# Output stage of three selective-scan layers: two passes with tokens on partitions in place of three stages with channels on partitions

## The chip, the cores and the metric

The kernel runs on one core of a Trainium2 chip. Its work is spread over five engines that take their instructions in order and wait for each other by semaphores: TensorE (PE in the profile, its weight loads PEld), VectorE (DVE), ScalarE (ACT), GpSimd (POOL) and SyncE (SP), which here issues all DMA transfers. The metric is the device time of one execution in microseconds (us). The kernel before was run three times outside the profiler.

## What is computed

The input is four images of 64 x 64 tokens with 192 channels, all float32. Four residual layers follow each other. Each normalizes the image by groups of channels, runs a selective state-space scan in one or four directions, and adds its result to the image. Layers b, c and d (the reference's L1, L2, L3) end alike. This is the part that the change touches, here of layer d (the sum is over its four directions; layer b has one):

```python
xz = jnp.einsum('bhwc,dc->bhwd', x, in_proj_w)
xc, z = jnp.split(xz, 2, axis=-1)
...
y = y1 + inv2 + wh + invwh
y = jnp.transpose(y, (0, 2, 1)).reshape(b, h, w, D_INNER)
mu = jnp.mean(y, axis=-1, keepdims=True)
var = jnp.var(y, axis=-1, keepdims=True)
y = (y - mu) * jax.lax.rsqrt(var + EPS) * ln_gamma + ln_beta
y = y * silu(z)
return jnp.einsum('bhwd,cd->bhwc', y, out_proj_w)
```

The layer norm runs over the 384 inner channels (192 in layer c) of each token. Layer b reverses every second row of the image before its scan and again behind it ("snake"). Layer a has no layer norm and an output stage of its own (`out0`), which stays as it is.

## The kernel before, in words

`net` (L961) takes the images one after the other and each through the layers a, b, c, d, so the output stage of `layer` (L893) runs 12 times. An image has L = 4096 tokens, cut into NCH = 8 chunks of T = 512; a chunk is TB = 4 blocks of 128 tokens. Inner channels lie in nb blocks of P: 3 x 128 in layers b and d, 2 x 96 in layer c.

`layer` first loads the image and convolves it, then `scans` (L274) makes the states and writes each direction's output to HBM with tokens in rows (`store`, L605: `yo`). The output stage reads these back in three stages, each with tile pools of its own:

- `gather` (L685): for each chunk it loads the 512 tokens of every direction (L693, tiles `yi`, tokens on partitions), and PE turns them by transposes that add up in PSUM (L699), 4 per block and direction. ACT or DVE copy the sum to `y` (L706 to L711), with channels on partitions; the snake is undone in that copy.
- `layernorm` (L713): the mean over channels is a sum over partitions, so PE multiplies with a matrix of 1/n (L722, `mean_w` of L54 to L58). DVE subtracts it (L725), ACT squares (L726), PE makes the mean of squares (L729), `rsqrt` (L77) takes Ln and Exp on ACT (L81, L82) and one Newton step of four DVE operations (L83 to L86), on 128 x 512 elements per chunk. DVE multiplies by gamma and by the result (L735).
- `gate_out` (L739): loads the image again (L746), `normalize` (L118, operation at L121), PE projects the gate z (L753), ACT takes Silu (L757), DVE adds beta and multiplies (L758), PE projects out (L765), DVE adds the image (L769), SP stores (L770). Its weights are loaded at L947 to L951.

Every float32 matmul of 512 columns stands in the trace as two records; every transpose as one.

The program text is not the order of execution on an engine. A scheduler of the tile framework orders each engine's instructions beforehand from its own estimate of when they can run, and adds the waits; `keep` (L261) pins the order inside the scans, and `behind` (L61) makes an instruction follow given others. A tile with `bufs=2` has two buffers in turn, and the third user waits for the first to be done. A new pool's first user waits for all that used that memory before.

Of the kernel before, what the change touches and what calls it, by code (L numbers as in the profile page):

```python
# [16 lines left out]
L = H * W  # L17
# [22 lines left out]
def rows(ap):  # L40

    return ap.rearrange("p (r w) -> p r w", w=W)


class Net:
    def __init__(self, tc, d, const):
        self.tc, self.nc, self.d = tc, tc.nc, d
        self.pinned = {}
        nc = self.nc
        self.ident = const.tile([128, 128], F32, tag="ident", name="ident")  # L50
        make_identity(nc, self.ident)
        self.gmat = const.tile([HP, HP], F32, tag="gmat", name="gmat")
        nc.sync.dma_start(self.gmat, d["gmat"])
        self.mean_w = {}  # L54
        for p, n in ((128, 384), (96, 192)):
            m = const.tile([p, p], F32, tag=f"mean{n}", name=f"mean{n}")
            nc.vector.memset(m, 1.0 / n)
            self.mean_w[n] = m  # L58
# [626 lines left out]
    def gather(self, pool, pp, y, outs, P, nb, snake, key):  # L685

        nc = self.nc
        for ch in range(NCH):
            s = slice(ch * T, (ch + 1) * T)
            yt = []  # L690
            for i, o in enumerate(outs):
                t = pool.tile([128, TB, nb * P], F32, tag=f"yt{i}", bufs=2, name=f"yi_{key}{ch}{i}")
                nc.sync.dma_start(t, o[s].rearrange("(q p) c -> p q c", p=128))  # L693
                yt.append(t)
            for b in range(nb):
                ps = pp.tile([P, T], F32, tag="py", bufs=2, name=f"pg_{key}{ch}{b}")
                for i, t in enumerate(yt):
                    for q in range(TB):
                        nc.tensor.matmul(  # L699
                            ps[:, q * 128 : (q + 1) * 128], t[:, q, b * P : (b + 1) * P], self.ident,  # L700
                            start=i == 0 and q == 0, stop=i == len(yt) - 1 and q == TB - 1,
                            is_transpose=True,
                        )
                o, ps = rows(y[:, b, s]), rows(ps)
                if snake:
                    nc.scalar.copy(o[:, 0::2, :], ps[:, 0::2, :])  # L706
                    nc.scalar.copy(o[:, 1::2, ::-1], ps[:, 1::2, :])
                elif b % 2:
                    nc.vector.tensor_copy(o, ps)
                else:  # L710
                    nc.scalar.copy(o, ps)  # L711

    def layernorm(self, pool, pp, y, P, nb, gamma, key):  # L713

        nc = self.nc
        ones = self.mean_w[P * nb]
        for ch in range(NCH):
            s = slice(ch * T, (ch + 1) * T)
            k = f"{key}{ch}"
            pm = pp.tile([P, T], F32, tag="pm", bufs=2, name=f"pm_{k}")  # L720
            for b in range(nb):
                nc.tensor.matmul(pm, ones, y[:, b, s], start=b == 0, stop=b == nb - 1)  # L722
            sq = pool.tile([P, nb, T], F32, tag="sq", bufs=2, name=f"sq_{k}")
            for b in range(nb):
                nc.vector.tensor_tensor(y[:, b, s], y[:, b, s], pm, ALU.subtract)  # L725
                nc.scalar.activation(sq[:, b, :], y[:, b, s], AF.Square)  # L726
            pv = pp.tile([P, T], F32, tag="pv", bufs=2, name=f"pv_{k}")
            for b in range(nb):
                nc.tensor.matmul(pv, ones, sq[:, b, :], start=b == 0, stop=b == nb - 1)  # L729
            v = pool.tile([P, T], F32, tag="v", bufs=2, name=f"v_{k}")  # L730
            nc.vector.tensor_scalar(v, pv, LN_EPS, None, ALU.add)
            r = pool.tile([P, T], F32, tag="r", bufs=2, name=f"r_{k}")
            self.rsqrt(pool, r, v, [P, T], k)
            for b in range(nb):
                nc.vector.scalar_tensor_tensor(  # L735
                    y[:, b, s], y[:, b, s], gamma[:, b, :], r, ALU.mult, ALU.mult
                )

    def gate_out(self, pool, pp, y, P, nb, wz, wo, beta, x_src, norm, dst, key):  # L739

        nc = self.nc
        for ch in range(NCH):
            s = slice(ch * T, (ch + 1) * T)
            k = f"{key}{ch}"
            x = pool.tile([HP, 2, T], F32, tag="gx", bufs=3, name=f"gx_{k}")
# [3 lines left out]
            o = pool.tile([P, nb, T], F32, tag="go", bufs=2, name=f"go_{k}")  # L749
            for b in range(nb):  # L750
                pz = pp.tile([P, T], F32, tag="pz", bufs=3, name=f"pz_{k}{b}")
                for h in range(2):
# [3 lines left out]
                z = pool.tile([P, T], F32, tag="gz", bufs=3, name=f"gz_{k}{b}")  # L756
                nc.scalar.activation(z, pz, AF.Silu)  # L757
                nc.vector.scalar_tensor_tensor(  # L758
                    o[:, b, :], y[:, b, s], beta[:, b, :], z, ALU.add, ALU.mult
                )  # L760
            res = pool.tile([HP, 2, T], F32, tag="gr", bufs=3, name=f"gr_{k}")
            for h in range(2):
                po = pp.tile([HP, T], F32, tag="po", bufs=2, name=f"po_{k}{h}")
                for b in range(nb):
                    nc.tensor.matmul(  # L765
                        po, wo[:, b, h * HP : (h + 1) * HP], o[:, b, :],
# [126 lines left out]
    def layer(self, name, x_src, dst, dp, P, nb, dirs, snake, twice):  # L893
# [5 lines left out]
        with tc.tile_pool(name=f"{name}_keep", bufs=1) as keep, ExitStack() as late:  # L899
# [154 lines left out]
```

## Time and profile before

| what | us |
|---|---|
| three runs, median (lowest to highest) | 35676.95 (35669.4 to 35704.8) |
| the profiled execution's own time | 35697.36 |
| span of the program in that execution | 35695.6 |
| output stage of layer b, four images: last transposed sum of the scan to last addition of L769 | 205.1, 206.1, 206.3, 208.9 |
| layer c, the same | 173.6, 175.3, 173.4, 173.6 |
| layer d, the same | 247.6, 248.0, 248.2, 246.8 |
| sum of these twelve | 2512.9 |
| mean granted TensorE clock over the span | 0.813 |

A profile shows one execution. Per group of equal instructions it gives the time they kept the engine busy, the mean of one in ns, and the idle time just before them with what ended it. A view by windows gives each engine's busy time in stretches of the span; beside it "PEclk" is the share of full clock that TensorE was granted, "DMA share" the mean busy share of the 16 DMA engines. A timeline lists instructions by start; runs of the same kind are merged ("x12"). A view of one source line gives shortest, median and longest duration of what this line issued. "a<-b,c" reads: written a, read b and c.

### The profile page before, as it was taken

To read this page: it belongs to the slowest core of one execution; us is meant where nothing else is said; L and a number is where in the kernel's file an instruction comes from. 1 tells how busy PE (TensorE), PEld (TensorE's weight loads), DVE (VectorE), ACT (ScalarE), POOL (GpSimd) and SP (SyncE) were. 2 spreads that over 40 slices of the span, in tenths; PEclk is the share of its full clock that TensorE was granted. 3 is DMA by queue.
4 is the path that set the end of the run, shared out by engine and by line. 5 is a ranking of instruction groups with operands and counts; after the bars stand their busy time and mean duration, and the time that the engine had idled before them with its cause. 6 is when DMAs were issued, how large, how long until landed. Compare 5 with 4: busy or idle time off the path is not lost. (4 is left out here: it accounts for less than half of the span.)

```text
span 35695.6 us, 396533 instructions
## 1 busy us (share of the span) xinstructions
PE 25702.0 (72%) x138688; PEld 18685.0 (52%) x138688; DVE 28265.2 (79%) x22866; ACT 24090.2 (67%) x45011; POOL 25347.8 (71%) x10978
## 2 busy tenths in 40 slices
PE   7778777666777877766677787776667778777666
PEld 4554454554455445455445544545544554454555
DVE  7885697887788569788778856978877885697887
ACT  6773585775677358577667735857766773585776
POOL 6883595896688359588668835958866883595886
PEclk8888877878888877787888887778788888777878
DMA  3332233223333223322333322332233332233223
GB/s 107 106 106 76 76 106 89 93 95 103 105 106 105 76 75 106 89 92 95 103 106 107 105 76 76 106 89 92 95 102 106 106 106 76 75 106 90 93 95 101
DMA packets 1354910, 3405.80 MB, mean 95 GB/s; under 512 B 185696, under 2 KB 633040, under 8 KB 1346768
## 3 DMA queue, kind: packets, MB, share of 16 engines
q1 hardware_dynamic: 1352912, 3380.43, 30.1%
q8 instruction: 1099, 18.01, 0.2%
q14 instruction: 899, 7.36, 0.1%
HBM read 2924.88 MB, written 455.08 MB: 95 GB/s over the span
## 5 line engine op out<-in xcount | busy, mean ns | idle before, releaser
L600 PE MATMUL py_d<-ident,c_d 128*128 128x128 f32 x24576 | 3823.1, 314 | 2138.6 <-POOL c_d L582 1307.7
L600 PE MATMUL py_a<-ident,c_a 128*128 128x128 f32 x24576 | 3635.0, 302 | 2212.5 <-POOL c_a L582 1143.6
L582 POOL TENSOR_TENSOR c_d<-h_d,C_d 128x1024 f32<-128x1024 f32 x2036 | 4777.0, 2366 | 163.2 <-DVE h_d L565 160.6
L582 POOL TENSOR_TENSOR c_a<-h_a,C_a 128x1024 f32<-128x1024 f32 x1908 | 4479.3, 2371 | 418.0 <-issue 284.2
L600 PEld LDWEIGHTS py_d<-ident,c_d 128*128 128x128 f32 x24576 | 3369.2, 164 | 2590.2 <-POOL c_d L582 1627.4
L600 PEld LDWEIGHTS py_a<-ident,c_a 128*128 128x128 f32 x24576 | 3155.4, 157 | 2522.0 <-DVE c_a L582 1267.7
L527 POOL TENSOR_TENSOR u_d<-du_d,B_d 128x1024 f32<-128x1024 f32 x1536 | 3618.4, 2360 | 900.0 <-issue 886.4
L527 POOL TENSOR_TENSOR u_a<-du_a,B_a 128x1024 f32<-128x1024 f32 x1536 | 3606.5, 2363 | 716.2 <-DVE h_a L558 696.5
L582 POOL TENSOR_TENSOR c_c<-h_c,C_c 96x1024 f32<-96x1024 f32 x1356 | 3179.2, 2361 | 383.4 <-DVE h_c L565 371.5
L565 DVE TENSOR_TENSOR_SCAN h_d<-dA_d,carry_d,u_d 128x512 f32<-128x512 f32 x2536 | 3073.3, 1264 | 333.3 <-POOL c_d L582 263.0
L519 ACT ACTIVATE dA_d<-delta_d,A_d 128x512 f32<-128x512 f32 x3072 | 2118.2, 690 | 1637.6 <-DVE c_d L582 1491.9
L519 ACT ACTIVATE dA_a<-delta_a,A_a 128x512 f32<-128x512 f32 x3072 | 2120.3, 690 | 1244.9 <-DVE c_a L582 1089.1
L600 PE MATMUL py_c<-ident,c_c 96*128 96x96 f32 x16384 | 2233.3, 303 | 867.3 <-DVE c_c L582 666.5
L558 DVE TENSOR_TENSOR_SCAN h_a<-dA_a,u_a 128x1024 f32<-128x1024 f32 x1140 | 2579.4, 2281 | 332.0 <-ACT dA_a L523 179.0
L600 PEld LDWEIGHTS py_c<-ident,c_c 96*128 96x128 f32 x16384 | 2025.9, 181 | 1196.9 <-DVE c_c L582 789.2
L527 POOL TENSOR_TENSOR u_c<-du_c,B_c 96x1024 f32<-96x1024 f32 x1024 | 2412.3, 2362 | 6.3 <-DVE dA_c L565 6.0
L544 PE MATMUL ut_d<-ident,dut_d 128*128 128x128 f32 x12288 | 1911.4, 307 | 631.5 <-DVE c_d L582 605.6
L536 ACT ACTIVATE dut_a<-duT_a,BT_a 128x384 f32<-128x384 f32 x4096 | 2291.9, 604 | 0.0
L536 ACT ACTIVATE dut_d<-duT_d,BT_d 128x384 f32<-128x384 f32 x4096 | 2290.7, 601 | 0.0
L565 DVE TENSOR_TENSOR_SCAN ut_d<-dAs_d,carry_d,ut_d 128x512 f32<-128x512 f32 x1536 | 1971.0, 1283 | 387.9 <-issue 167.9
L519 ACT ACTIVATE dAs_d<-delta_d,A_d 128x512 f32<-128x512 f32 x3072 | 2043.0, 713 | 296.6 <-DVE h_d L565 230.3
L544 PEld LDWEIGHTS ut_d<-ident,dut_d 128*128 128x128 f32 x12288 | 1586.1, 158 | 1147.2 <-issue 946.4
(366 smaller groups left out, 64427.4 us busy)
## 6 DMA issues: line engine op xcount, KB each, us to landing
C_a<-bc_a SPq DMA_DIRECT2D x1024, 512.0 KB
C_d<-bc_d SPq DMA_DIRECT2D x1024, 512.0 KB
C_c<-bc_c SPq DMA_DIRECT2D x1024, 384.0 KB
B_a<-bc_a SPq DMA_DIRECT2D x512, 512.0 KB
B_d<-bc_d SPq DMA_DIRECT2D x512, 512.0 KB
B_c<-bc_c SPq DMA_DIRECT2D x512, 384.0 KB
C_b<-bc_b SPq DMA_DIRECT2D x256, 512.0 KB
xd_a<-xo_a SPq DMA_DIRECT2D x48, 2048.0 KB
```

What stands on the lines that cost most here:

```text
L519: keep(nc.scalar.activation(out, delta, AF.Exp, scale=o.A[:, t.b, k : k + 1]))
L527: keep(nc.gpsimd.tensor_tensor(t.u, t.c.du[:, t.b, None, :].to_broadcast([P, NT, T]), t.c.B[t.j], ALU.mult))
L536: keep(nc.scalar.activation(c.scaled[n][:, q, :], c.duT[:, q, :], AF.Copy, scale=c.BT[:, q, n : n + 1]))
L544: keep(nc.tensor.transpose(t.u[:, n, q * 128 : (q + 1) * 128], t.c.scaled[t.n0 + n][:, q, t.b * P : (t.b + 1) * P], self.ident,))
L558: keep(nc.vector.tensor_tensor_scan(hf, af, uf, 0.0, ALU.mult, ALU.add))
L565: keep(nc.vector.tensor_tensor_scan(hf, af, uf, o.carry[:, t.b, k : k + 1], ALU.mult, ALU.add))
L582: keep(engine.tensor_tensor(t.cm, t.h, t.c.C[t.j], ALU.mult))
L600: keep(nc.tensor.matmul(c.py[b][:, q, :], t.cm[:, n, q * 128 : (q + 1) * 128], self.ident[:P, :P], start=first, stop=c.sums[b] == NS and q ...
```

## The change

The three stages of layers b, c and d become one function, `output`, with two passes over the chunks. It keeps tokens on partitions until the layer norm is applied.

First pass, per chunk: load the directions' outputs, the first into `y` (32 blocks of 128 tokens, kept); add the other three in SBUF, two additions on DVE and one on POOL; `bn_stats` and `bn_aggr` on DVE give mean and variance of each token; load the image, normalize it, project the gate, and keep Silu of it in `z`. Then, once for all tokens, `rsqrt` on a 128 x 32 tile, behind all gates. Second pass, per chunk: DVE subtracts the mean and multiplies by the reciprocal deviation, both per partition; PE turns the result; ACT evicts it with gamma and beta as per-partition scale and bias; POOL multiplies by the gate; PE projects out; the image is loaded once more and added; SP stores. `xc` has a pool of its own now that ends with the scans; the 1/n matrices are gone.

```diff
-        self.mean_w = {}
-        for p, n in ((128, 384), (96, 192)):
-            m = const.tile([p, p], F32, tag=f"mean{n}", name=f"mean{n}")
-            nc.vector.memset(m, 1.0 / n)
-            self.mean_w[n] = m
...
+    def output(self, pool, pp, P, nb, outs, wz, wo, ln, snake, x_src, norm, dst, key):
+        nc = self.nc
+        n = P * nb
+        y = pool.tile([128, NCH * TB, n], F32, tag="y", name=f"y_{key}")
+        z = pool.tile([P, nb, L], F32, tag="z", name=f"z_{key}")
+        mv = pool.tile([128, NCH * TB, 2], F32, tag="mv", name=f"mv_{key}")
+        gates = []
+        for ch in range(NCH):
+            s = slice(ch * T, (ch + 1) * T)
+            k = f"{key}{ch}"
+            parts = []
+            for i, o in enumerate(outs):
+                t = y[:, ch * TB : (ch + 1) * TB, :]
+                if i:
+                    t = pool.tile([128, TB, n], F32, tag=f"yt{i}", bufs=2, name=f"yi_{k}{i}")
+                nc.sync.dma_start(t, o[s].rearrange("(q p) c -> p q c", p=128))
+                parts.append(t)
+            if len(parts) > 1:
+                nc.vector.tensor_tensor(parts[0], parts[0], parts[1], ALU.add)
+                nc.gpsimd.tensor_tensor(parts[2], parts[2], parts[3], ALU.add)
+                nc.vector.tensor_tensor(parts[0], parts[0], parts[2], ALU.add)
+            for q in range(ch * TB, (ch + 1) * TB):
+                st = pool.tile([128, 6], F32, tag="st", bufs=4, name=f"st_{key}{q}")
+                nc.vector.bn_stats(st, y[:, q, :])
+                nc.vector.bn_aggr(mv[:, q, :], st)
+            x = pool.tile([HP, 2, T], F32, tag="gx", bufs=2, name=f"gx_{k}")
+            nc.sync.dma_start(x, x_src[:, :, s])
+            xn = pool.tile([HP, 2, T], F32, tag="gn", bufs=2, name=f"gn_{k}")
+            self.normalize(xn, x, norm)
+            for b in range(nb):
+                pz = pp.tile([P, T], F32, tag="pz", bufs=3, name=f"pz_{k}{b}")
+                for h in range(2):
+                    nc.tensor.matmul(
+                        pz, wz[:, h, b * P : (b + 1) * P], xn[:, h, :], start=h == 0, stop=h == 1
+                    )
+                gates.append(nc.scalar.activation(z[:, b, s], pz, AF.Silu))
+        v = pool.tile([128, NCH * TB, 1], F32, tag="v", name=f"v_{key}")
+        nc.vector.tensor_scalar(v, mv[:, :, 1:2], LN_EPS, None, ALU.add)
+        r = pool.tile([128, NCH * TB, 1], F32, tag="r", name=f"r_{key}")
+        with self.behind(gates):
+            self.rsqrt(pool, r, v, [128, NCH * TB, 1], key)
+        for ch in range(NCH):
...
+            for q in range(ch * TB, (ch + 1) * TB):
+                nc.vector.tensor_scalar(
+                    y[:, q, :], y[:, q, :], mv[:, q, 0:1], r[:, q, :], ALU.subtract, ALU.mult
+                )
+            g = pool.tile([P, nb, T], F32, tag="g", bufs=2, name=f"g_{k}")
+            for b in range(nb):
+                py = pp.tile([P, T], F32, tag="py", bufs=3, name=f"pg_{k}{b}")
+                for q in range(TB):
+                    nc.tensor.matmul(
+                        py[:, q * 128 : (q + 1) * 128], y[:, ch * TB + q, b * P : (b + 1) * P],
+                        self.ident, start=q == 0, stop=q == TB - 1, is_transpose=True,
+                    )
+                o, v = rows(g[:, b, :]), rows(py)
+                gamma, beta = ln[:, b, 0:1], ln[:, b, 1:2]
+                for o, v in (
+                    ((o[:, 0::2, :], v[:, 0::2, :]), (o[:, 1::2, ::-1], v[:, 1::2, :]))
+                    if snake else ((o, v),)
+                ):
+                    nc.scalar.activation(o, v, AF.Identity, scale=gamma, bias=beta)
+                nc.gpsimd.tensor_tensor(g[:, b, :], g[:, b, :], z[:, b, s], ALU.mult)
+            x = pool.tile([HP, 2, T], F32, tag="gx", bufs=2, name=f"gy_{k}")
+            nc.sync.dma_start(x, x_src[:, :, s])
+            res = pool.tile([HP, 2, T], F32, tag="gr", bufs=2, name=f"gr_{k}")
+            for h in range(2):
+                po = pp.tile([HP, T], F32, tag="po", bufs=2, name=f"po_{k}{h}")
+                for b in range(nb):
                     nc.tensor.matmul(
-                        po, wo[:, b, h * HP : (h + 1) * HP], o[:, b, :],
+                        po, wo[:, b, h * HP : (h + 1) * HP], g[:, b, :],
                         start=b == 0, stop=b == nb - 1,
                     )
                 nc.vector.tensor_tensor(res[:, h, :], po, x[:, h, :], ALU.add)
             nc.sync.dma_start(dst[:, :, s], res)
```

In `layer` the weights `ln`, `wz` and `wo` are now loaded ahead of the first direction's output, in the one pool that serves both passes.

## The prediction, made before the changed kernel was run

> **What bounds the kernel now.** I first asked the page for the chain of work that ended last. It covers only the last few instructions (every share is 0%), so it says nothing. The page's busy rows say that no engine is full:
>
> ```profile
> PE 25702.0 (72%) x138688; PEld 18685.0 (52%) x138688; DVE 28265.2 (79%) x22866; ACT 24090.2 (67%) x45011; POOL 25347.8 (71%) x10978
> ```
>
> The scans make most of that. The layers are serial: each starts with the mean of the whole image that the one before stored. So a microsecond won in an output stage is won at the end, unless the start of the next layer changes. I therefore cut the first image's output stages into gather, layer norm and gate by the view of windows (columns: stretch, length, busy time of each engine, granted clock, DMA share, GB/s), layers b, c, d in turn:
>
> ```profile
> 3901.80:3939.70 37.90, 20.34 (x97) 15.73 (x97) 0.00 (x0) 15.91 (x49) 0.00 (x0) 0.66 0.59 187
> 3939.70:4011.50 71.80, 47.96 (x96) 18.58 (x96) 53.88 (x88) 45.50 (x56) 0.00 (x0) 0.87 0.00 0
> 4011.50:4106.90 95.40, 85.84 (x192) 34.82 (x192) 36.48 (x56) 15.61 (x25) 0.00 (x0) 0.92 0.25 68
> 5842.40:5890.70 48.30, 35.85 (x256) 29.93 (x256) 5.49 (x8) 5.13 (x9) 0.00 (x0) 0.82 0.91 270
> 5890.70:5951.10 60.40, 34.20 (x64) 10.55 (x64) 44.30 (x72) 40.14 (x48) 0.00 (x0) 0.78 0.00 0
> 5951.10:6016.00 64.90, 57.12 (x128) 20.46 (x128) 29.97 (x48) 10.76 (x17) 0.00 (x0) 0.92 0.35 96
> 8658.20:8739.40 81.20, 51.98 (x386) 44.14 (x385) 5.54 (x8) 9.95 (x17) 0.00 (x0) 0.89 0.93 320
> 8739.40:8811.10 71.70, 47.75 (x96) 18.67 (x96) 53.95 (x88) 45.50 (x56) 0.00 (x0) 0.87 0.00 1
> 8811.10:8905.80 94.70, 86.05 (x192) 34.85 (x192) 36.48 (x57) 15.61 (x25) 0.00 (x0) 0.92 0.26 69
> ```
>
> Gather in c and d is DMA (share 0.91, 0.93); the layer norm moves no data and fills no engine, a chain DVE, ACT, PE; the gate is PE. POOL is idle throughout. Two timelines of layer d give the paces, gather first (start, length):
>
> ```profile
> 8694.11 0.58 ACT L711 COPY y_d<-pg_d 128x512 f32<-128x512 f32 x1 [5.21 <-PE pg_d L699]
> 8699.73 1.09 PE L699 MATMUL pg_d<-ident,yi_d 128*128 128x128 f32 x8 [0.81 <-DMA yi_d<-yo_d]
> 8702.52 0.59 ACT L711 COPY y_d<-pg_d 128x512 f32<-128x512 f32 x1 [5.18 <-PE pg_d L699]
> ```
>
> A chunk takes 8.41 us (8702.52 - 8694.11) for 4 x 786 KB = 3.15 MB, 374 GB/s. Eight transposes in 1.09 us, less the pipelined end of the last, come 0.107 us apart. In the gate stage:
>
> ```profile
> 8868.88 5.32 PE L765 MATMUL po_d<-go_d,wo_d 128*96 128x512 f32 x12
> 8874.03 5.31 PE L753 MATMUL pz_d<-gn_d,wz_d 96*128 96x512 f32 x12
> 8879.18 5.32 PE L765 MATMUL po_d<-go_d,wo_d 128*96 128x512 f32 x12
> ```
>
> Twelve records (six matmuls) every 5.15 us without a gap: 0.86 us a matmul, 10.3 us a chunk, 82.4 us for eight.
>
> **First pass.** Removed: the layer norm's 12 matmuls a chunk, its ACT and DVE work, its 16 table loads a stage, and the gate's wait of 7.2 us for weights (8811.1 to 8818.3). Per chunk it now holds:
> - DMA, d: 8.41 + 0.393 MB of image at 374 GB/s = 1.05, 9.5 us. c: transposes ran from 5850.4 to 5889.9, 4.95 a chunk; + 1.05 = 6.0. b: 1.18 MB, 3.2 us at that rate.
> - PE: the gate, 5.15 us in b and d, 3.44 in c (four matmuls).
> - DVE: two additions in d and c, statistics, two normalizations. Rows for their durations:
>
> ```profile
> L582 DVE TENSOR_TENSOR c_d<-ut_d,C_d x768: 1214/1214/1217, 6223.3 to 35441.5; 128x1024 f32<-128x1024 f32 x192
> L423 POOL TENSOR_TENSOR du_b<-delta_b,xc_b x32: 3417/3460/3518, 3273.7 to 30570.0; 128x1536 f32<-128x1536 f32 x32
> L121 DVE TENSOR_SCALAR gn_d<-gx_d,mean_d,rstd_d x64: 534/541/544, 8818.3 to 35666.6; 96x512 f32<-96x512 f32 x64
> ```
>
> 1214 ns for 1024 columns and 681 for 512 (L725) make 1.04 ns a column plus 0.15. An addition of 1536 is 1.74 us, 1.66 from start to start. `bn_stats` has no row. Low end: one read per column, 384 x 1.04 + 0.15 = 0.55, 0.46 start to start; high end: two walks, 0.95; I take 0.5, as every DVE row here with one output per column reads it once. `bn_aggr` on six columns is like L575 on two: 0.16. d: 3.3 + 4 x 0.46 + 4 x 0.12 + 0.94 = 6.6 us; c: 4.2; b: 3.3. At the high end d has 8.4 of 9.5, c 5.1 of 6.0, b 5.1 of 5.15: still covered, and only the last chunk's tail is longer by 2 us.
> - POOL: one addition, 3.5 us in d.
>
> So the first pass is DMA in c and d and PE in b. DVE's second addition waits for POOL's, and behind it on DVE queue the statistics and the normalization that PE needs; as DMA sets the pace with 3 us to spare, only the last chunk shows it. On SP the image load of chunk k+2 waits for the normalization of chunk k (two buffers), and the later chunks' loads stand behind it; it is free 7.4 us after chunk k landed, when transfers for 2 us more are queued. The second pass loads the image again, beside a DMA share of 0.26 in the gate stage: hidden; uncovered it would be 1.05 us a chunk.
>
> Sum for d from the scan's end: before, the eight chunks had landed after about 79 us (the last transpose ends at 80.5); add the weights, now ahead of `y` on SP (0.59 MB, 1.6 us), and 8 x 1.05: 89. Tail: POOL's addition ends 2.5 us later (the image lands last), DVE's 4.2, the second normalization 7.4, the gate's last matmuls 10.1 (11.5 at a low clock), Silu 12.2. Then Ln and Exp on 32 columns with two table loads of 1.28, and four small DVE operations: 3.8, and four normalizations by token, 1.6: transposes can go at 89 + 17.5. [...] Before, each of L81 and L82 has a load of its own in every chunk (8 and 8 in layer d's stage, 1283 ns). [...]
> c: 46 + 0.8 + 8.4 = 55, tail 13 (shorter additions and statistics). b: first gate at 12 us (before, first transpose at 8.8; weights and image come ahead), 8 x 5.15 + 2.6 for the low clock at the start = 56, tail 6.
>
> **Second pass.** PE: 12 transposes (1.3 us) and six matmuls = 6.45 us a chunk, 51.5 for eight (c: 0.86 + 3.44 = 4.3). DVE's 32 normalizations (0.2 + 0.27 from L121's 541 for 512 columns and 2406 for 4096: 0.47) run ahead of PE. ACT is 0.6 per block. POOL's multiplication, 512 columns: the scans' 2363 for 1024 and 3460 for 1536 give 1.26; three are 3.8 us a chunk, covered. But it adds a link: PE, ACT, POOL, PE, and g comes 1.26 us apart. In the changed program's order PE turns five blocks, does one chunk's projection, turns two, does the next. In the first of such a pair PE turns for 1.7 us, the first g is there at 2.5, the second at 3.8, the third at 5.0: 1.6 us of standing; 0.3 in the second. Pair 14.7 us; with first and last chunk alone (8.4 each): 61, with POOL at 1.26 62. c: 42.5, b: as d.
>
> [...] I take 1.5 of 0 to 7, and 2 us for the low clock behind PE's idle tail. Last addition: 0.9.
>
> **Sum.** d: 89 + 17.5 + 62 + 3.5 = 172 of 247.6 (mean); won 75.5. b: 62 + 61 + 3.5 + 0.9 = 127 of 206.6; 79. c: 55 + 13 + 42.5 + 3.5 = 114 of 174.0; 60. The next layer's loads are ordered as before behind the last store: 0. Four images x 214.5 = 857 us. The profiled execution took 35697.4, so 34840; the median is 20 lower: 34820. Own range 34720 to 34920 (both ends of `bn_stats`, lock, clock: about 8 us a stage).
>
> **Rivals.**
> 1. PE's waits hide (the order lets POOL run ahead, tails overlap): 10 us fewer in pass 2 and 5 in the tail, 15 x 12 = 180: 34640. For: POOL is idle half the time. Chance 0.13.
> 2. [...] Chance 0.20.
> 3. Slower: `bn_stats`, the one operation without a row, is many passes. DVE then bounds pass 1. With p its pace, DVE per chunk of d, b, c is 4.7 + 4p, 1.4 + 4p, 3.2 + 4p against 9.5, 5.15, 6.0; 8 x (12p - 11.3) eats the 214.5 us at p = 3.2. At 4 us: 8 x 36.7 - 214.5 = 79 us an image, 35990. Against: six times the addition's rate. Chance 0.03.
> 4. The gain is given back elsewhere, within 0.2%: 0.02.
>
> The likeliest has 0.62. Range 34630 to 35080: to about the middle of rivals 1 and 2, so half of each is left out, and cases 3 and 4, some 2 in 10. Faster by over 0.2% (71 us, about what this measurement can tell from no change) 0.95, within 0.02, slower 0.03.
>
> **What will show it.** Layer d's stage 172 us, its first pass at DMA share over 0.9 and near 9.5 us a chunk; `bn_stats` 0.5 us; in layer b the gate's matmuls without gaps; in pass 2 PE waiting for `g` from POOL about 1 us a chunk. I am wrong if DVE fills pass 1, if POOL's product takes over 2 us from ready to done, or if PE stays at half clock through pass 2 (6.45 us more a chunk).

## The result, and the profile after

The kernel after takes 35046.4 us (median of four runs, 35025.3 to 35059.0), beside 35685.2 us for the kernel before in the same session: a ratio of 0.982, 95% interval 0.9803 to 0.9837. That is 639 us won where 857 were forecast. The profiled executions, 35697.4 before and 35048.6 after, differ by 649.

The page of the kernel after again fills no engine; its busy row answers the one shown of before:

```profile
PE 25072.0 (72%) x135744; PEld 18264.5 (52%) x135744; DVE 27941.2 (80%) x22892; ACT 23687.5 (68%) x44483; POOL 25888.4 (74%) x11298
```

The windows of the first image, cut where the passes meet (first transpose of the normalized rows), for b, c and d, and a steady part of d's first pass last. Columns are as before: stretch, length, busy time of each engine, clock, DMA share, GB/s.

```profile
3902.00:3968.00 66.00, 44.60 (x97) 19.42 (x97) 27.12 (x87) 19.22 (x30) 0.00 (x0) 0.81 0.69 176
3968.00:4045.50 77.50, 62.70 (x192) 28.02 (x192) 22.98 (x47) 22.73 (x48) 37.08 (x24) 0.86 0.24 66
5784.50:5862.60 78.10, 41.53 (x64) 13.09 (x64) 33.73 (x103) 14.26 (x22) 14.40 (x8) 0.70 0.86 221
5862.60:5912.60 50.00, 42.71 (x128) 18.42 (x128) 25.52 (x47) 11.31 (x16) 20.14 (x16) 0.89 0.36 103
8552.60:8679.60 127.00, 62.70 (x98) 24.91 (x97) 53.11 (x103) 19.11 (x30) 27.35 (x8) 0.72 0.84 240
8679.60:8756.50 76.90, 63.91 (x192) 27.54 (x192) 22.98 (x47) 16.91 (x24) 36.33 (x24) 0.89 0.23 67
8582.00:8640.00 58.00, 38.20 (x60) 14.97 (x59) 30.49 (x58) 10.13 (x16) 17.10 (x5) 0.78 1.07 309
```

The layer norm's stage with no transfers is gone. In the last row the DMA share is full (1.07), as forecast, but only 309 GB/s move where the gather of before moved 374. The means of the four images, against the forecast's own terms:

| stage | first pass, forecast / measured | second pass, forecast / measured | stage, forecast / measured |
|---|---|---|---|
| b | 62 / 66.3 | 65.4 / 76.7 | 127 / 143.0 |
| c | 68 / 80.6 | 46 / 50.5 | 114 / 131.1 |
| d | 106.5 / 123.4 | 65.5 / 76.8 | 172 / 200.2 |

The twelve stages took 2512.9 us before and take 1897.2, so 616 of the 649 us between the two spans lie in them. The remaining 33 us lie in the scans and convolutions, whose work the change leaves as it was; 20 of them are layer c's scan of the third image alone. The next section shows that they cannot be counted as a gain of the change.

**First pass.** The timeline of GpSimd in d shows its addition once a chunk (start, length):

```profile
8599.72 3.42 POOL L701 TENSOR_TENSOR yi_d<-yi_d,yi_d 128x1536 f32<-128x1536 f32 x1 [9.30 <-DMA yi_d<-yo_d]
8611.65 3.42 POOL L701 TENSOR_TENSOR yi_d<-yi_d,yi_d 128x1536 f32<-128x1536 f32 x1 [8.52 <-DMA yi_d<-yo_d]
8623.55 3.42 POOL L701 TENSOR_TENSOR yi_d<-yi_d,yi_d 128x1536 f32<-128x1536 f32 x1 [8.47 <-DMA yi_d<-yo_d]
```

It waits for the directions each time, and a chunk takes 11.9 us, not 9.5. The transfers' rate through that stretch (40 slices of 1.45 us) tells where the time goes:

```profile
GB/s 341 198 235 258 326 373 374 373 325 188 272 246 322 372 372 374 322 169 238 252 335 372 373 374 316 184 254 259 349 368 372 374 290 203 247 282 363 354 373 374
```

Once a chunk, while the image's 393 KB are under way, the rate falls to about half (169 to 203 GB/s, where it is 374 between).

**Second pass.** The timeline around the turn of d:

```profile
8675.04 1.28 ACT L76 ACT_TABLE_LOAD   x1
8676.58 1.28 ACT L77 ACT_TABLE_LOAD   x1
8679.03 6.71 DVE L727 TENSOR_SCALAR y_d<-y_d,mv_d,r_d 128x384 f32<-128x384 f32 x17
8682.18 7.13 POOL L745 TENSOR_TENSOR g_d<-g_d,z_d 128x512 f32<-128x512 f32 x3 [18.97 <-ACT g_d L744]
8686.92 8.38 PE L752 MATMUL po_d<-g_d,wo_d 128*96 128x512 f32 x12 [4.14 <-POOL g_d L745]
8695.95 3.97 DVE L727 TENSOR_SCALAR y_d<-y_d,mv_d,r_d 128x384 f32<-128x384 f32 x10
8696.52 8.18 POOL L745 TENSOR_TENSOR g_d<-g_d,z_d 128x512 f32<-128x512 f32 x4 [7.21 <-ACT g_d L744]
8701.09 3.73 PE L752 MATMUL po_d<-g_d,wo_d 128*96 128x512 f32 x4 [3.94 <-POOL g_d L745]
```

The reader should set the rows of VectorE and GpSimd side by side. Seventeen normalizations run to 8685.74. The first product starts at 8682.18, and PE, which waits for it, goes on at 8686.92: the product took 4.7 us and ended one product's length after the normalizations did. The same happens again at 8696. Over d's four images the shortest, median and longest (ns) are:

```profile
L745 POOL TENSOR_TENSOR g_d<-g_d,z_d x96: 1254/1262/4686, 8682.2 to 35036.9; 128x512 f32<-128x512 f32 x96
```

### The profile page after: what moved, and what is told of

Read it like the earlier page. It is cut to its first block, busy times and chain, and to the rows that moved or that the text cites. A ratio compares the mean times of both kernels' runs of the same rounds, so it can differ in the third digit from the quotient of the medians.

```text
span 35046.5 us, 390536 instructions
## 1 busy us (share of the span) xinstructions
PE 25072.0 (72%) x135744; PEld 18264.5 (52%) x135744; DVE 27941.2 (80%) x22892; ACT 23687.5 (68%) x44483; POOL 25888.4 (74%) x11298
```

## The experiments

My theory after this reading: the structure of the forecast holds, and three of its terms were too small: the image load in the first pass, GpSimd's hold-up in the second, and the weights ahead of the first chunk. The rival: VectorE, with its statistics and additions, or the chain PE, ACT, POOL, PE sets the pace, and the rate of the transfers is only a consequence. A kernel that was run once shows its time to about 20 us either way (the four runs of the kernel after span 34 us). The scans between the stages differ from profile to profile as well: in each of the twelve kernels below they took 15 to 54 us longer in all than in the profile of after, 7 to 24 us of it in c's scan of the third image. So the 33 us just named are not shown to belong to the change, and I judge by the stages. These scatter too: two tiles, product on VectorE and one table leave the first pass alone, but for one table's shorter turn at its end, and have it at 117.4 to 121.1 us in d and 75.4 to 80.3 in c, where after has 123.4 and 80.6. The table has means over the four images, in us: first pass, second pass.

| kernel | b | c | d | twelve stages | time |
|---|---|---|---|---|---|
| after | 66.3, 76.7 | 80.6, 50.5 | 123.4, 76.8 | 1897 | 35046.4 |
| dense source | 66.8, 77.1 | 78.7, 48.9 | 120.5, 76.3 | 1873 | 35044.2 |
| image once | 66.2, 76.6 | 59.6, 49.1 | 98.1, 75.9 | 1702 | 34886.3 |
| two tiles | 66.0, 66.0 | 80.3, 51.9 | 119.9, 68.3 | 1809 | 34997.7 |
| statistics twice | 68.5, 76.0 | 79.2, 49.3 | 123.4, 76.3 | 1891 | 35096.0 |
| product on VectorE | 66.6, 57.3 | 77.2, 39.4 | 121.1, 57.6 | 1677 | 34853.4 |
| gates late | 41.0, 110.7 | 59.0, 68.4 | 95.9, 110.8 | 1944 | 35120.9 |
| 128 partitions | 66.2, 75.6 | 70.6, 49.8 | 104.5, 76.5 | 1773 | 34964.7 |
| weights later | 63.1, 77.2 | 78.2, 49.8 | 115.6, 76.0 | 1840 | 35027.5 |
| both | 63.0, 57.2 | 79.7, 39.5 | 115.7, 57.6 | 1651 | 34845.8 |
| split image | 118.5, 58.0 | 80.8, 40.0 | 116.1, 57.1 | 1882 | 35074.3 |
| one table | 65.2, 75.2 | 75.4, 44.9 | 117.4, 75.2 | 1814 | 34989.5 |
| full rows | 61.8, 57.8 | 78.8, 39.3 | 112.6, 56.8 | 1629 | 34793.4 |

The kernel before took 35680.8 us beside the four runs from "dense source" to "statistics twice", 35689.3 beside the next four, and 35705.3 (both, split image, one table) and 35693.4 (full rows) beside the last.

### What sets the first pass

**Image once.**

```diff
-            x = pool.tile([HP, 2, T], F32, tag="gx", bufs=2, name=f"gx_{k}")
-            nc.sync.dma_start(x, x_src[:, :, s])
+            if ch == 0:
+                x = pool.tile([HP, 2, T], F32, tag="gx0", name=f"gx_{k}")
+                nc.sync.dma_start(x, x_src[:, :, s])
```

> The image is loaded only for chunk 0 of the first pass, and every chunk's gates are made from it, so 7 of 8 first-pass image loads are gone and every other instruction stays. Theory A (loads set the first pass): stage d's pace falls from 11.9 us to what the directions alone took in the gather of before, 8.4 us, so d loses 7 x 3.5 = 25 us an image, c falls to its directions' 4.2 us or to its gate matmuls' 5.2, whichever is longer, 7 x 1.8 = 13 us, b is bound by its gate matmuls and keeps its stage within 2 us: 4 x 38 = 150 us in all, 34,895 us. Theory B (the additions, with GpSimd's 3.4 us behind VectorE, or the queue's issue set the pace): d's pace stays above 11 us and the time within 20 us of 35,046.

Measured: d's chunks came 8.46 us apart (median; 11.61 in after), and its first pass fell by 25.3 us to 98.1. The forecast without its eight image loads is 89 + 17.5 - 8.4 = 98.1. So the other terms of the first pass were right in sum, though one load stays here and the gates no longer come last, so that the exact agreement is luck. c fell by 21, more than expected, b by nothing. So one image load costs d 3.15 us a chunk by the pace and 25.3 / 7 = 3.6 with what is saved at the end of the pass, and c 2.4 and 3.0, where 1.05 was forecast.

**Statistics twice.**

```diff
                 nc.vector.bn_stats(st, y[:, q, :])
+                nc.vector.bn_stats(st, y[:, q, :])
```

> Each bn_stats is issued twice, 32 more of 0.54 us in each image of stage d, of 0.54 in b (as its row of 384 columns has) and of 0.33 in c. Theory A (the statistics are hidden: behind the loads in d and c, behind the gate matmuls in b): d and c keep their pace, each stage is longer only by its last chunk's four more, 2.2 us, and b by no more than that: 4 x (2.2 + 2.2 + 1.3) = 23 us at most, 35,047 to 35,070 us. Theory B (VectorE is what paces the first pass): each chunk is longer by its four, 2.2 us in d and b and 1.3 us in c: 4 x 8 x 5.7 = 182 us, 35,230 us.

Measured: d's first pass is unchanged (123.4), c's shorter by 1.4, b's longer by 2.2. The time is 50 us above the kernel after, more than either the tails or the stages explain: the stages together are 6 us shorter, and the rest lies in scans that the edit does not touch (37 us of it in c's). So statistics of 0.53 us could be doubled at no cost to c and d; VectorE does not bound the first pass, and the rival falls there.

**Dense source**, which asks why the load is slow: by where it reads, or where it writes.

```diff
-            nc.sync.dma_start(x, x_src[:, :, s])
+            flat = outs[0][s].rearrange("t c -> (t c)")[: HP * 2 * T]
+            nc.sync.dma_start(x, flat.rearrange("(k p t) -> p k t", k=2, p=HP))
```

> The first-pass image load keeps its size, its destination (96 partitions) and its place in the queue, but reads 393 KB that lie together in a direction's output instead of rows that lie 16 KB apart in the image; the gates are therefore made from other data. Theory A (the source's stride makes the load slow, 145 ns a packet of 2 KB): packets of this load fall to about 85 ns, and stage d's first pass goes from 11.9 us a chunk to about 9.5 to 10, which takes 8 x 2 = 16 us from stage d and about 6 from c, some 90 us from the kernel in all (34,960 us). Theory B (what makes it slow is the writing side, 96 partitions of 2 KB beside 128 of 1.5 KB): the pace stays within 0.4 us of 11.9 and the time within 20 us of 35,046.

Measured: packets of 2 KB took 137 ns instead of 145 (mean in d's first image; 132 instead of 137 over all four), and the pace went from 11.6 us (median of all four images) to 11.35. Theory A falls: it asked for 9.5 to 10, and 0.26 us is no more than the pace moves in kernels that leave this load alone (11.1 in one table, 11.3 in two tiles).

**128 partitions**, against the kernel with the dense source (the normalization's own lines are left out of the cut; it reads two overlapping pieces of the tile).

```diff
-            x = pool.tile([HP, 2, T], F32, tag="gx", bufs=2, name=f"gx_{k}")
+            x = pool.tile([128, 2, 384], F32, tag="gx", bufs=2, name=f"gx_{k}")
...
-            nc.sync.dma_start(x, flat.rearrange("(k p t) -> p k t", k=2, p=HP))
+            nc.sync.dma_start(x, flat.rearrange("(k p t) -> p k t", k=2, p=128))
```

> The dense source of before (an output of a direction), and the same 393 KB, but written to 128 partitions as two packets of 1,536 bytes each instead of to 96 partitions as two of 2,048; the normalization takes overlapping pieces of it, so the gates are made from other data. [...]

Measured: d's pace 9.51 us and c's 5.87 (medians), the forecast's 9.5 and 6.0. The rate in d (40 slices of 1.63 us) has no dips left until the loads end:

```profile
GB/s 371 375 378 365 377 368 373 374 372 372 375 373 372 375 372 372 374 373 372 373 373 372 373 374 371 374 373 372 373 373 372 374 374 371 374 374 372 372 290 210
```

So in d the same bytes in 1.5 KB pieces to all 128 partitions cost 9.51 - 8.46 = 1.05 us, the forecast's figure, and to 96 partitions 11.35 - 8.46 = 2.9, nearly three times that. This run changes more than the partitions: the pieces are smaller, and the second pass's image has buffers of its own. "Full rows" below has pieces of 2 KB again, to all partitions in sum; they took 100 to 107 ns each (means of d's four images), where after has 132 to 145, and the pace was 10.1. So the size explains the smaller part at most. Why 96 partitions are slower is not shown.

**Weights later.** The three parameter loads become a function that `output` calls behind the first chunk's four direction loads.

```diff
                 parts.append(t)
+            if ch == 0:
+                weights()
...
-                nc.sync.dma_start(wz, w_in[:, :, inner:])
...
+                def weights():
...
+                    nc.sync.dma_start(wz, w_in[:, :, inner:])
```

> The three loads of the layer norm's parameters, gate weights and output weights are issued behind the first chunk's four direction loads instead of ahead of them. Theory A (they stand ahead of the first chunk for more than the 1.6 us forecast): in d the first addition starts 2 to 3 us earlier, and since loads set d's first pass only if the total falls, d keeps its stage (the bytes are the same); in b the gates, which are the bound there, start no earlier either, because they wait for the same loads in another order: within 15 us of 35,046. Theory B (the weights' short rows of 768 B and 1.5 KB are slow only when nothing else is in flight, and overlap with the directions otherwise): each of the 12 stages is 2 to 4 us shorter, 34,995 to 35,020.

Measured: b's first pass is 3.2 us shorter, c's 2.4, d's 7.8, and the stages are 57 us shorter in sum; the time fell by only 19, which one run can hardly tell from nothing. Theory A's claim that nothing is won fails in b, where the first gate starts 2.9 us earlier (mean) and every image gains, and in d, where it starts 2.8 us earlier. In c it starts no earlier, and 2.4 us lie within the scatter. The other 5 us of d lie in the pace, 11.2 us against 11.6; one table, which loads in the old order, has 11.1, so they are not shown to come from this edit.

**Gates late**, which undoes one part of the change: the second pass makes the gates.

```diff
-            xn = pool.tile([HP, 2, T], F32, tag="gn", bufs=2, name=f"gn_{k}")
-            self.normalize(xn, x, norm)
...
+            x = pool.tile([HP, 2, T], F32, tag="gx", bufs=3, name=f"gy_{k}")
+            nc.sync.dma_start(x, x_src[:, :, s])
+            xn = pool.tile([HP, 2, T], F32, tag="gn", bufs=2, name=f"gn_{k}")
+            self.normalize(xn, x, norm)
```

> This undoes one part of the change: the gates are made in the second pass, from the one image load that it has anyway, so the first pass has no image load, no image normalization and no gate matmuls. Theory A (the first pass's gates are hidden in b, and cost d and c only their image load): the first pass loses what loading the image once took away, about 25 us an image in d, 21 in c, and some 10 in b, where the loads' 8.4 us a chunk are replaced by nothing shorter than the gather itself; the second pass gains the gate matmuls, 5.2 to 5.6 us a chunk in b and d and about 3.5 in c, 43, 43 and 28 us an image. Net: 4 x (33 + 18 + 7) = 230 us slower, 35,280 us, with 35,150 to 35,400 allowed. Theory B (the gates' place is worth nothing, because what the second pass gains the first gives back in loads): within 40 us of 35,046.

Measured: 74 us slower than after, 47 of it in the stages: +8.8 an image in b, -3.7 in c, +6.6 in d. Both theories miss. The second pass grew by 34 us in b and d and 18 in c, less than the gates' 43 and 28, because PE now fills its waits with them. The first pass fell by 27.5 in d and 21.6 in c as expected, and in b by 25 instead of 10: without gates b is bound by nothing but one direction's loads, and I had put the four directions' 8.4 us a chunk there. So gates in the first pass, with their own slow image load, are worth 47 of the 616 us; the rest lies in the other parts of the change (sums and statistics with tokens on partitions, one `rsqrt` for all), which no run here took apart.

### What sets the second pass

**Two tiles.**

```diff
+                if q % TB == 0:
+                    yn = pool.tile([128, TB, n], F32, tag="yn", bufs=2, name=f"yn_{k}")
...
-                    y[:, q, :], y[:, q, :], mv[:, q, 0:1], r[:, q, :], ALU.subtract, ALU.mult
+                    yn[:, q % TB, :], y[:, q, :], mv[:, q, 0:1], r[:, q, :], ALU.subtract, ALU.mult
...
-                        py[:, q * 128 : (q + 1) * 128], y[:, ch * TB + q, b * P : (b + 1) * P],
+                        py[:, q * 128 : (q + 1) * 128], yn[:, q, b * P : (b + 1) * P],
```

> The second pass writes the normalized rows of a chunk to one of two small tiles instead of back into the large one, so VectorE can be at most two chunks ahead of the turning. Theory A (the first half of the second pass is slow because VectorE runs 17 and then 10 normalizations in a row, during which GpSimd's product takes 2 us instead of 1.26): the normalizations come eight at a time, TensorE's idle 4.1 and 3.9 us in the first chunks shrink to under 1.5 each, and each of b and d loses 4 to 6 us an image, c 2 to 3: 40 to 60 us in all, 34,990 to 35,005 us. Theory B (the same normalizations lock GpSimd out wherever they lie, so the loss is only spread): the sum of TensorE's waits for the product in the second pass stays as it is, and the time stays within 15 us of 35,046.

Measured: 10.7 us less in b's second pass, 8.5 in d's, 1.4 more in c's. The timeline of d shows the mechanism:

```profile
8673.12 3.21 DVE L729 TENSOR_SCALAR yn_d<-y_d,mv_d,r_d 128x384 f32<-128x384 f32 x8
8676.27 3.95 POOL L747 TENSOR_TENSOR g_d<-g_d,z_d 128x512 f32<-128x512 f32 x3 [17.27 <-ACT g_d L746]
8676.69 4.13 DVE L729 TENSOR_SCALAR yn_d<-y_d,mv_d,r_d 128x384 f32<-128x384 f32 x4 [0.37 <-PE pg_d L736]
8677.59 1.10 PE L754 MATMUL po_d<-g_d,wo_d 128*96 128x512 f32 x2 [0.77 <-POOL g_d L747]
```

The three products take 3.95 us, not 7.13, and PE's wait is 0.77, not 4.14. Now four normalizations take 4.13 us where eight took 3.21: the hold-up goes the other way, onto an engine that has time. PE's instructions in d stand in the same order in both kernels, but PE waits less here, and its clock differs with that. The third ten us of d's second pass, in after and then here:

```profile
8699.60:8709.60 10.00, 8.51 (x17) 3.38 (x18) 1.35 (x3) 0.00 (x0) 5.10 (x4) 0.66 0.01 3
```

```profile
8693.70:8703.70 10.00, 8.71 (x32) 3.53 (x30) 7.71 (x8) 3.84 (x6) 5.27 (x5) 1.00 0.51 145
```

The granted clock is 0.66 to 0.67 behind the long waits and 1.00 behind the short ones, in all four images, and the output matmuls of the second chunk take 839 to 849 ns a record in after, 612 here. Theory A holds for b and d; the gain is twice my figure, and c, whose products were never longer than 2.0 us, has none.

**Product on VectorE.**

```diff
-                nc.gpsimd.tensor_tensor(g[:, b, :], g[:, b, :], z[:, b, s], ALU.mult)
+                nc.vector.tensor_tensor(g[:, b, :], g[:, b, :], z[:, b, s], ALU.mult)
```

> The gate's product in the second pass goes from GpSimd to VectorE, and the planner lays the second pass out anew; GpSimd has nothing there, so no normalization can hold it up. Theory A (what the second pass loses is GpSimd's product behind VectorE's normalizations): as with two tiles, b and d each lose 11 to 12 us an image, and since the product is about 0.7 us here and not 1.26, TensorE's remaining waits of 0.7 and 1.4 us a chunk shrink as well: 12 to 16 us an image in b and d, 2 to 5 in c, 110 to 150 us in all, 34,900 to 34,940. Theory B (VectorE gets the stalls instead: the product now stands behind up to seventeen normalizations of 0.47 us in its own queue): b and d gain under 6 us an image, 35,000 or more.

Measured: 19.4 us less in b's second pass, 11.1 in c's, 19.2 in d's. PE's groups in d's second pass, of after and then of this kernel (busy, mean ns, idle before):

```profile
L752 PE MATMUL po_d<-g_d,wo_d 128*96 128x512 f32 x96 | 51.5, 671 | 12.1 <-POOL g_d L745 10.8
```

```profile
L752 PE MATMUL po_d<-g_d,wo_d 128*96 128x512 f32 x96 | 44.1, 610 | 0.7 <-DVE g_d L745 0.7
```

The wait of 10.8 us is gone, and the matmuls are shorter as well: PE hardly idles, and the mean clock of the pass is 0.95 instead of 0.89. So in the second pass GpSimd's product cost twice: by its waits (10.8 us beside 0.7), and by the clock behind them (671 ns a matmul record beside 610). This one line is worth 193 us by one run, 220 by the stages. Product and order changed together here, since the planner also laid PE's and VectorE's instructions out anew; two tiles is the run that keeps PE's order.

**One table.** One instruction per stage, behind the last gate.

```diff
         with self.behind(gates):
+            self.keep(nc.scalar.preload_act_table_set(NLE))
             self.rsqrt(pool, r, v, [128, NCH * TB, 1], key)
```

> One instruction more per stage: behind the last gate ScalarE loads the table that holds both Ln and Exp, ahead of the variance's Ln. [...] Theory B (Ln and Exp are loaded apart whatever has been loaded before): a third load of 1.28 us is added and the turn is as long or longer, 35,046 to 35,065.

Measured, in d's timeline of ScalarE:

```profile
8664.20 1.28 ACT L722 ACT_TABLE_LOAD   x1
8665.49 0.23 ACT L76 ACTIVATE rsq_d<-v_d 128x32 f32<-128x32 f32 x1
8665.75 0.23 ACT L77 ACTIVATE r_d<-rsq_d 128x32 f32<-128x32 f32 x1
```

Ln and Exp follow one load of 1.28 us; the kernels before and after, which do not ask for that set here, get a load of 1.28 us before each. The turn from last gate to first transpose is 3.9 us instead of 5.2. c gained 10.8 us an image, far more than 1.3; 5.6 of it lie in its second pass. The second image's second pass in c, of after and then of this kernel:

```profile
14631.30:14681.30 50.00, 42.78 (x128) 18.41 (x128) 25.53 (x47) 11.31 (x16) 20.10 (x16) 0.89 0.36 103
```

```profile
14607.90:14653.10 45.20, 41.50 (x128) 18.66 (x128) 24.84 (x47) 11.19 (x16) 20.38 (x16) 0.90 0.40 114
```

The clock is the same within 0.01, and PE stands still for 3.7 us instead of 7.2. In the first image this kernel has a clock of 0.97 in the pass, in the other three 0.89 to 0.90 (after: 0.83 to 0.89); yet the first gains 5.5 us, no more than the mean. What differs in all four is the planner's order: here PE alternates between 16 transposes and 16 records of projections throughout, where after begins with 11 transposes, 8 records, 13 transposes. The six other kernels that have after's gates and product keep after's order, and none of them takes less than 48.9 us (mean of four images). So the likely cause is the new order and not the shorter pause; the order was not tried alone. The first passes of c and d are also 5 to 6 us shorter, of which the turn explains 1.3; most of the rest lies in their pace (11.1 us a chunk in d, 7.1 in c), for which I have no cause.

### Together

**Both** has the product on VectorE and the weights later.

> The product of the second pass on VectorE and the three parameter loads behind the first chunk's directions, together; nothing is left out. Theory A (the two act in different stretches and add up): the stages lose the 220 us and the 57 us that they lost apart, so 35,046 - 277, with the scans as they were in most profiles some 20 us longer: 34,770 to 34,800 us. Theory B (the earlier start is given back where loads set the pace): no better than the product alone, 34,840 to 34,860.

Measured: 34845.8 us (34825.5 to 34850.8), ratio to before 0.9758 (0.9741 to 0.9774). By the time this is Theory B's figure, by the stages it is nearer Theory A: they lost 246 us of the 277, and the scans took 23 us longer than in the profile of the product alone. The stages add up for b (63.0 and 57.2, as apart) and for d, and c's first pass is 2.5 us longer than with the product alone, within the scatter.

**Split image** adds to "both" another cut of the real image.

```diff
+            x = pool.tile([128, T], F32, tag="gxa", bufs=2, name=f"gx_{k}")
+            nc.sync.dma_start(x, rows192[:128, s])
+            lo = slice(64 * (ch % 2), 64 * (ch % 2) + 64)
+            if ch % 2 == 0:
+                nc.sync.dma_start(xb[:64], rows192[128:, s])
+                nc.sync.dma_start(xb[64:], rows192[128:, (ch + 1) * T : (ch + 2) * T])
...
+                nc.tensor.matmul(pz, wz[:, 0, b * P : (b + 1) * P], xn, start=True, stop=False)
+                nc.tensor.matmul(pz, wz[lo, 1, b * P : (b + 1) * P], xm[lo], start=False, stop=True)
```

> As the run with both, and the first pass loads the real image in another cut: channels 0 to 127 to 128 partitions, and channels 128 to 191 of two chunks to partitions 0 to 63 and 64 to 127; gate weights, means and deviations are laid out to match (eight small loads more per stage and a third more gate weights), TensorE contracts 128 and 64 channels instead of 96 and 96, and the output is the reference's. Theory A (only the 96 partitions made the load slow): d's pace falls from 11.3-11.6 us to about 9.5-9.8, c's from 7.4 to about 6, as with 128 partitions and other data, which was worth 43 us in c and 77 us in d: 34,650 to 34,690 us, and the first chunk's extra loads cost up to 2 us a stage, 25 us. [...]

Measured: 35074.3 us (35049.2 to 35084.8), ratio 0.9823 (0.9808 to 0.9837): all that "both" had won over after is lost, by something that Theory A did not have. d's pace did fall to about 10.1 us. But b's first pass went from 63 to 118.5. The windows of b's first pass, of "both" and then of this kernel:

```profile
3920.00:3960.00 40.00, 39.27 (x86) 17.35 (x87) 23.47 (x73) 13.82 (x22) 0.00 (x0) 0.93 0.77 214
```

```profile
3930.00:4010.00 80.00, 80.00 (x81) 19.96 (x80) 16.30 (x51) 11.94 (x20) 0.00 (x0) 0.50 0.22 63
```

PE is busy nearly throughout in both, and the granted clock is 0.93 and 0.50: it stayed at half for the 96 us of the gates, in all four images.

**Full rows** contracts 128 rows always, with weights that are zero in the other chunk's half, in c and d only, and takes the one table.

```diff
+                    xm = pool.tile([128, T], F32, tag="gm", bufs=2, name=f"gm_{k}")
...
+                terms = [(wz[:, 0, :], xn), (wz[:, 1 + ch % 2, :], xm)]
```

> The run with both, plus the table that holds Ln and Exp loaded behind the last gate, plus the other cut of the first pass's image in c and d only: channels 0 to 127 to 128 partitions, channels 128 to 191 of two chunks to partitions 0 to 63 and 64 to 127, and here every gate matmul contracts all 128 rows: its second weights are zero in the half of the rows that belongs to the other chunk. Nothing is left out. Theory A (in the run before, the half clock of 0.50 that doubled b's first pass and bounded d's came with the contractions of 64 rows, and the loads themselves were mended): the clock is as without the cut, d's pace is 9.5 to 9.8 us a chunk and c's about 6, b is as in the run with both less 1.3 us of its turn; d loses 8 x 1.6 = 13, c 8 x 1.2 = 10, and each turn 1.3: 4 x (13 + 10 + 4) = 108 us under 34,846, 34,740 us, and 34,700 to 34,780 allowed. Theory B (the loads to 64 partitions are as slow as those to 96): d's pace stays above 10.8 and only the turns gain, 34,820 to 34,840. Theory C (the clock falls again, for the cut's sake): the gates at 2 us a pair bound d and c, 34,850 or more.

Measured: 34793.4 us (34776.1 to 34797.0), ratio to before 0.9746 (0.9732 to 0.9759); it is the fastest, some 250 us under the kernel after, and short of Theory A's 34740, just outside the range allowed to it. Theory B asked for a pace above 10.8, Theory C for the low clock. The clock in d is 0.81, so the half clock does not come with every such cut. The steady pace in d is 10.0 to 10.1 us and c's median 6.56, a little over theory A. Most of what is missing lies at the start, in the transfers' rate from the first chunk (40 slices of 0.6 us):

```profile
GB/s 374 376 369 374 371 376 371 342 296 314 260 243 76 1 0 1 0 34 222 331 190 125 172 375 404 376 381 399 392 396 361 369 371 381 371 375 379 378 377 372
```

For some 3 us nothing moves: eight loads of 0.1 to 0.4 KB for means and deviations take SP 0.6 us each to issue, with two waits of about 1.6 us between, and the second chunk stands behind them. The first interval in d is 17 to 19 us, against 12 to 14 in "both". I had costed them at 2 us.

## Why the prediction was right in kind and short in size

The forecast's range and sign held; its likeliest time was 226 us too low, so that the measured one lies outside that case's own range of 34720 to 34920. The stages ran 245 us over their forecast (4 x (16.0 + 17.1 + 28.2)), and outside them 33 us were won that no step had; the difference, 212, stands for the 218 by which the 639 us won fall short of 857 (the profiles differ by 649, and the stages' forecasts are rounded). That the time fell inside the range is in part luck: no rival had the slow image load, which made half of the miss, and the 33 us outside the stages are not shown to be the change's. The measured time lies near the slow end of the range of 34630 to 35080: GpSimd's product is held up (4.69 us for the first of d, where the median is 1.26), while long tails from the statistics do not show (doubled, they leave d's first pass at 123.4 us).

**What held.** The layer norm's stage of 60 to 72 us is gone; how the time won divides over the parts of the change was not measured. b's first pass is its gate matmuls: PE is busy 44.60 of 66.0 us in the windows, all the time from the first gate to the last, and statistics doubled change little. d's first pass has a DMA share of 1.07 in its steady part. The operation without a row was measured: `bn_stats` 530 ns against 0.5 us, which ends rival 3, and `bn_aggr` 160 ns. Normalizations take 474 ns, POOL's additions 3.42 us, its product alone 1.26, all as costed. The two table loads are as the row had them, and one load is enough once the set is asked for: 1.3 us a turn. The "12 matmuls a chunk" of the layer norm are twelve records, so six matmuls; no sum used them.

**First step that failed: "8.41 + 0.393 MB of image at 374 GB/s = 1.05, 9.5 us".** A rate from loads to 128 partitions was given to a load to 96. It costs 3.15 us a chunk in d and 2.4 in c by the paces, so that a chunk of d takes 11.6 us. The trace of before had a nearer row, which I passed over: the load of the next image by layer a, 3.15 MB to 96 partitions, from 8908.97 (rate in 40 slices of 0.425 us from 8908):

```profile
GB/s 82 5 0 0 77 77 154 337 279 299 231 222 280 212 260 241 241 251 212 251 289 231 241 231 270 241 222 280 270 231 270 260 231 231 225 258 259 196 257 259
```

Its packets fill 13.7 us, 230 GB/s, with nearly nothing else under way until its last two us. At that rate the image costs 1.7 us a chunk, which would have given 10.1 in d, a third of the way to 11.6. The runs show that most of the difference is 96 against 128 partitions (2.9 us a chunk in d beside 1.05); why it is nearly threefold stays open. Price: about 17 us a stage in d and 13 in c, some 120 us of the 245.

**Second: "I take 1.5 of 0 to 7, and 2 us for the low clock behind PE's idle tail".** The 1.5 us was my estimate of what VectorE's normalizations cost by holding up GpSimd's product, the "lock" of the forecast's own range. No run shows that term; in its place the kernel after showed a first product of 4.69 us that ended 1.1 us behind the last of 17 normalizations, and 10.8 us in which PE waited for products in d's pass of the first image. By the forecast's own sign, a product of over 2 us from ready to done, this step was wrong. VectorE gets ahead more than once (17, then 10), and behind PE's waits its clock falls to 0.73 in 8680 to 8702; the second chunk's matmul records, which start there, take 839 to 849 ns, and 612 in two tiles. Two tiles give back 8.5 to 10.7 us in b and d, so the forecast's 3.5 us for hold-up and low clock were nearer 10; that is 5 to 7 of the 11.3 us by which each pass ran over. The rest, 4 to 6 us, was not taken apart. In c two tiles gave nothing, yet PE stood still for 7 of its 50 us, and with the product on VectorE the pass took 39.4: there PE's waits behind the link through GpSimd cost, or the order around them, and not the runs of normalizations. Price: 4 x (11.3 + 11.3 + 4.5) = 108 us.

**Third, small: weights "1.6 us".** In b the first gate starts at 16.2 to 17.1 us behind the scan's end, not at 12. With the weights later it starts at 13.3 to 14.4. Price: some 4 us in b.

The prices are the measured excess of each pass laid on one step each, so they sum to it: 120 + 108 + 17 = 245. The experiments took most of each away: 128 partitions 16 to 19 us in d and 8 to 10 in c (against the dense source and against after), the product on VectorE more than the whole of the second.

## What to carry to other kernels

Cost a transfer by a row with the same number of partitions, and not by the best rate in the trace: here 96 partitions made the same bytes nearly three times as dear as 128 (2.9 us a chunk beside 1.05). When a cheap operation moves to an idle engine, ask what the busy one queues beside it; where each holds the other, as here (a product of 4.69 us for 1.26, four normalizations in 4.13 us where eight took 3.21), bound how far one may run ahead, or keep the product on the engine that does the rest. And a wait of TensorE was paid twice here, once as a wait and again in the clock that followed: in the first chunks of d's second pass, 4.14 and 3.94 us of waiting and a clock of 0.66 to 0.67 behind them, where behind the short waits of two tiles it was 1.00.

## What the hardware showed that I had not expected

- VectorE and GpSimd held each other up in both directions: GpSimd's product took 4.69 us beside 17 normalizations, where the median is 1.26, and in two tiles four of VectorE's normalizations took 4.13 us, where eight had taken 3.21. In "full rows" most of d's image normalizations, 0.55 us alone, take about 3.0 (median), one of them while GpSimd adds:

```profile
8554.57 3.12 DVE L723 TENSOR_SCALAR gn_d<-gx_d,mean_d,rstd_d 128x512 f32<-128x512 f32 x1 [3.99 <-DMA gx_d<-x]
8554.00 3.42 POOL L713 TENSOR_TENSOR yi_d<-yi_d,yi_d 128x1536 f32<-128x1536 f32 x1 [14.70 <-DMA yi_d<-yo_d]
```

- Every second matmul contracting 64 rows, with PE busy throughout, went with a clock of 0.50 for 96 us in b. In d of the same kernel it was 0.71 in the steady part, and with 128 rows 0.81. Whether the 64 rows or the alternation is the reason was not tried alone.
- An ACT copy with scale and bias per partition took 776 ns for 512 columns, where Silu of the same size took 597.
